# A Mamba layer and its experts on one core: input with channels on rows, the skip term on GpSimd, TensorE busy before its first weights

## The chip, the cores and the metric

The kernel runs on one core of a Trainium2 chip, in one launch and in fp32. The metric is the device time of an execution in microseconds (us), the median over several runs. A profile is of one execution. Engines: PE (TensorE), DVE (VectorE), ACT (ScalarE), POOL (GpSimd) and SP (SyncE, which issues most DMAs). Each works off its own queue of instructions in order, and waits at an instruction until what it needs is there.

## What is computed

Input x is 4 sequences of 1024 tokens with 128 channels. Cut to what matters:

```python
# Mamba: 256 inner channels, 16 states, rank 64, causal convolution over 4 tokens
xr, z = split(x @ W_in.T)                # 256 and 256
xs    = silu(conv(xr, conv_w) + conv_b)
dt_r, b, c = split(xs @ W_x.T)           # 64, 16, 16
dt    = softplus(dt_r @ W_dt.T + b_dt)
for t in range(1024):                    # for each channel and each of 16 states
    h = exp(dt_t * -exp(A_log)) * h + dt_t * xs_t * b_t
    y_t = sum over states (h * c_t) + D * xs_t        # D * xs_t: the skip term
x = layernorm(x + (y * silu(z)) @ W_out.T)
# 8 experts of 128 -> 512 -> 128 with gelu, the best 2 of each token, softmax weights
x = layernorm(x + sum over the 2 experts e of weight_e * expert_e(x))
```

## The kernel before

**Units.** The 4096 tokens are cut into ten units, each a stretch of one sequence: two of 256, then 512s, and at the end 384 and 128 (`UNITS`; units 0 to 9). A unit has its tokens along the free axis and the inner channels on rows, as two halves of 128 (index c). If a unit continues a sequence, the state of the recurrence is carried in a small tile (`goes_on`).

**prepare** of a unit runs during the scans of the unit before. `load_x` (L441) brings x with tokens on rows. `project` (L577) transposes it on PE with the identity into PSUM (`pt_x`, L585), and ACT copies it to `xt` (L603), a tile with 3 extra columns in front for the convolution (the halo: zeros at the start of a sequence, else copied from the unit before by ACT, L595). The convolution is folded into the projection: the four taps times W_in (`taps`, multiplied on DVE, L326) are the weights of four matmuls that accumulate in `pxc` (L613); silu on ACT gives `xs`. `pz` (L638) and its silu `zs` (L649) follow. `select` (L658) makes `px`, `xd`, the transposed b (`bt`), c through DRAM (`cd`), `pd` and the first parts of softplus (`ex`); `softplus` (L732) ends it with a polynomial (`sq` on ACT, `q` four times on DVE), then `dt` and `dtx` = dt * xs on DVE.

**step** (L802), 16 a unit, one for each state: PE spreads b over the rows into PSUM (`u`, L824); a DMA spreads c over the rows of `cc`; ACT makes the decay `a`; DVE multiplies dtx by the spread b (`u`, L861) and runs two scans, one for each half (`h`, L880, two buffers of both halves); POOL multiplies by c (`hc`, L895, three buffers); PE transposes hc and accumulates it over the states into `y` in PSUM (L905, tokens on rows); POOL copies the last state where the sequence goes on (`state`, L920).

**The skip term** (`add_skip`, L926) is ahead of the first state's transposes: PE multiplies xs by a diagonal matrix of D (`skip_sb`, made on DVE at the start, L348), 64 matmuls in all (128 records in fp32), and so starts y's accumulation (L937).

**finish_mixer** (L945) multiplies y by zs (`yg`), projects with W_out (`po`), adds x and normalizes (`stats_m`, `rstd_m`), and makes the routing.

**Experts.** Sparse rounds 0 to 7 take units (0,1), 2, 3, ... 8; the last unit is computed densely, with all experts. `dispatch` (L1113) works out on DVE which slot each token takes, ending with its weights (`twin`, L1241), and POOL scatters the tokens to slots in DRAM with indirect DMAs (`xs_slots`, L1262), eight for a unit of 512. `experts` (L1322) reads slots back four blocks of 128 at a time (`xb`), transposes them (`pt_b`), moves them to `xq`, runs both layers (`ph`, `ht`) with weights that each block's expert selects, and weighs the result (`yb`), which a DMA writes out. In rounds below `LATE` ACT makes `xq` (L1350) and `yb` (L1426), from `LATE` on DVE does (L1359, L1428). `combine` (L1484) gathers on POOL (L1495) and adds; `store` normalizes and writes.

**Order.** A planner (`Plan`, L77) lists all operations with an estimated cost, a wished place and an urgency, and `order` (L147) simulates the engines with these estimates to fix the sequence of each engine's queue; `issue` writes it out as it stands. The constants at the top of the file (`UP`, `GATHER`, `PREP_OF`, `D_OF` and others) are its costs and wishes, so to change them changes the order and nothing else.

**At the start**, x of unit 0 is loaded first, the identity is made on POOL, W_in (256 KB) and the taps are loaded, and PE's first instructions are the transposes of x.

Of the kernel before, what the change touches and what calls it, by code (L numbers as in the profile page):

```python
# [18 lines left out]
RUSH = 100.0  # L19
NEAR, LOTH = 0.1, 1.3  # L20

UP = 0.95
GATHER, SCATTER = 1.85, 1.35
N_B = 2
SCAN_ORDER = 1, 0
B_AT, B_URG = 3.6, 29.9
BESIDE = -6.2
PATIENCE = 0.2
N_RUSH = 0
X_AT, X_STEP, X_URG, C_AT, C_URG, D_AT = 1.9, 2.66, 6.2, 4.0, -1.0, -1.9  # L30
A_AT, A_URG, BC_AT, BC_URG = -0.8, -2.3, 4.2, 15.8
PREP, SEL, SOFT, SSTEP = 25.4, 5.3, -0.1, 2.7
L_URG = -1.0
URG, URG2, URG3, URG4 = 52.0, 191.1, 18.3, 0.8
Z_AT, W2_AT, W1_AT, W1_STEP = 11.2, 0.0, 6.8, 3.5

PREP_OF = (-6.7, -1.0, -10.0, 9.5, 1.2, 0.0, -3.0, 5.6, -5.2, 6.9, -3.9, 3.0)
D_OF = (7.9, -3.5, -6.5, 3.3, 6.5, 4.7, -8.1, 5.3, 4.5, 1.7)
X_OF = (-1.9, -7.6, 2.1, 1.3, 0.5, 0.4, 0.8, -16.1, 6.0, -2.5)
C_OF = (-0.2, 5.0, -3.5, -1.3, 8.3, 3.3, 21.1, -2.6, 2.7, 9.1)  # L40
# [5 lines left out]

DENSE = [(9,)]

LATE = 7
EPS = 1e-5  # L50
TOPK = 2

# [199 lines left out]
def tile_mamba_moe_postln(  # L252
# [18 lines left out]
    out: bass.AP,  # L271
):
    nc = tc.nc
    _, _, DM = x.shape
    KC, DI = conv_w.shape
    NS = a_log.shape[0]
    RK = w_dt_t.shape[0]
# [23 lines left out]
    ps_m = ctx.enter_context(tc.tile_pool(name="ps_m", bufs=5 - N_B, space=bass.MemoryType.PSUM))  # L301


    x_first = io.tile([P, NTC, DM], F32, tag="x", name="x_0", bufs=2)
    nc.sync.dma_start(
        out=x_first[:, : UNITS[0][2] // P, :],
        in_=x[0, : UNITS[0][2], :].rearrange("(c p) d -> p c d", p=P),
    )
    ident = const.tile([P, P], F32, name="ident")
    make_identity(nc, ident)  # L310
    w_in_sb = const.tile([P, 2 * DI], F32, name="w_in_sb")
    nc.sync.dma_start(out=w_in_sb, in_=w_in_t)
# [5 lines left out]
    for j, v in ((1, d_skip), (2, b_dt)):  # L318
# [4 lines left out]
    w_dt_sb = const.tile([RK, DI], F32, name="w_dt_sb")  # L323
    nc.sync.dma_start(out=w_dt_sb, in_=w_dt_t)

    nc.vector.tensor_tensor(  # L326
        taps, taps, w_in_sb[:, :DI].unsqueeze(1).to_broadcast([P, KC, DI]), ALU.mult
    )
# [17 lines left out]
    skip_sb = const.tile([P, NDC, P], F32, name="skip_sb")  # L346
    for c in range(NDC):
        nc.vector.tensor_scalar_mul(skip_sb[:, c, :], ident, vecs[:, 1, c : c + 1])  # L348
    ones = const.tile([P, P], F32, name="ones")
    nc.gpsimd.memset(ones, 1.0)  # L350

# [87 lines left out]
    )  # L439

    def load_x(i, st):  # L441
        b, r = rows(i)
        n = size(i)[1]
        st["x"] = t = sb(io, [P, NTC, DM], "x", 2, f"x_{i}")
        if i == 0:
            t.make = lambda: x_first
            dma(lambda: t(), (), [t], 128)
            return
        dma(
            lambda: nc.sync.dma_start(  # L450
                out=t()[:, :n, :], in_=x[b, r, :].rearrange("(c p) d -> p c d", p=P)
            ),
            (),
            [t],
            256,
        )

    def layernorm(src, part, n, name, *dst):

# [112 lines left out]
    dve(0, lambda: nc.vector.tensor_scalar_mul(nega, nega, -1.0), [decay], [decay])  # L572


    last_xt = {}

    def project(i, st):  # L577
        t_n, n = size(i)
        b, first, _ = UNITS[i]
        src = st["x"]  # L580
        pt = psum(f"pt_x{i}")

        def turn():
            for c in range(n):
                nc.tensor.transpose(pt()[:, c * P : (c + 1) * P], src()[:, c, :], ident)  # L585


        xt = sb(seq, [P, HALO + T], "xt", 3, f"xt_{i}")
        if first == 0:
            dve(0, lambda: nc.vector.memset(xt()[:, :HALO], 0.0), (), [(xt, "halo")], port=False)  # L590
        else:
            prev, end = last_xt[i - 1]
            act(
                0,
                lambda: nc.scalar.copy(xt()[:, :HALO], prev()[:, end : end + HALO]),  # L595
                [(prev, "body")],
                [(xt, "halo")],
            )
        last_xt[i] = xt, t_n
        pe(0.12 * n, turn, [src, (xt, "halo")], [pt])  # L600
        act(
            t_n,
            lambda: nc.scalar.copy(xt()[:, HALO : HALO + t_n], pt()[:, :t_n]),  # L603
            [pt],
            [(xt, "body")],
        )
        xs = sb(seq, [P, NDC, T], "xs", 1, f"xs_{i}")
        for c in range(NDC):
            pp = psum(f"pxc_{i}_{c}")

            def mm(c=c, pp=pp):
                for k in range(KC):
                    nc.tensor.matmul(  # L613
                        pp()[:, :t_n],
                        taps[:, k, c * P : (c + 1) * P],
                        xt()[:, k : k + t_n],
                        start=(k == 0),
                        stop=(k == KC - 1),
                    )

            pe(KC * 1.7e-3 * t_n, mm, [xt], [pp], holds=[xs])

            def fxs(c=c, pp=pp):
                nc.scalar.activation(
                    xs()[:, c, :t_n], pp()[:, :t_n], AF.Silu, bias=vecs[:, 0, c : c + 1]
                )

            act(t_n, fxs, [pp], [(xs, c)], SILU)

        zs = sb(seq, [P, NTC, DI], "zs", 2, f"zs_{i}")  # L630
        for h in range((n + 1) // 2):
# [24 lines left out]
        st["zs"], st["xs"], st["xt"] = zs, xs, xt  # L656

    def select(i, st):  # L658
        t_n, n = size(i)
# [142 lines left out]
    def step(i, st, s):  # L802
# [50 lines left out]
            place=place - A_AT,  # L853
            urgent=A_URG,
        )
        h = sb(scan, [P, NDC, T], "h", 2, f"h_{i}_{s}")

        dve(
            2 * t_n,
# [11 lines left out]
        )  # L871
        hc = sb(scan, [P, NDC, T], "hc", 3, f"hc_{i}_{s}")
        if s == 0:
            add_skip(i, st)
        y = st["y"]
        for c in SCAN_ORDER:

            def run(c=c):
# [15 lines left out]
            def times(c=c):  # L894
# [2 lines left out]
                )  # L897

            plan.add(
                "POOL", 0.05 + 2.33e-3 * t_n, times, [(h, c), cc], [(hc, c)], urgent=30.0, port=True  # L900
            )

            def add(c=c):
                for k in range(n):
                    nc.tensor.matmul(  # L905
                        y()[:, k, c * P : (c + 1) * P],
                        hc()[:, c, k * P : (k + 1) * P],
                        ident,
                        is_transpose=True,
                        start=False,  # L910
                        stop=(s == NS - 1),
                        skip_group_check=True,
                    )

            plan.add("PE", 0.12 * n, add, [(hc, c), y], [y], urgent=30.0)
        if goes_on:
            plan.add(
                "POOL",
                0.15,
                lambda: nc.gpsimd.tensor_copy(carry()[:, s, :], h()[:, :, t_n - 1]),  # L920
                [h],
                [(carry, s)],
                urgent=30.0,
            )


    def add_skip(i, st):
        n = size(i)[1]
        st["y"] = y = plan.buf(
            "y", 1, lambda: ps_y.tile([P, NTC, DI], F32, tag="y", name=f"y_{i}")  # L930
        )
        xs = st["xs"]

        def run():
            for k in range(n):
                for c in range(NDC):
                    nc.tensor.matmul(  # L937
                        y()[:, k, c * P : (c + 1) * P],
                        xs()[:, c, k * P : (k + 1) * P],
                        skip_sb[:, c, :],  # L940
                        start=(k % 2 == 0 and c == 0),
                        stop=False,
                        skip_group_check=True,
                    )

        plan.add("PE", 0.48 * n, run, [xs], [y], urgent=30.0)


    def finish_mixer(i, st, at):
# [534 lines left out]
    def combine(i, st, at):  # L1484
# [184 lines left out]
```

## Time and profile before

| | |
|---|---|
| median of 15 runs | 798.04 us (794.72 to 800.02) |
| profiled execution | 796.63 us, of which its span 794.9 us |
| mean clock granted to PE | 0.914 of full speed |
| instructions of PE, DVE, ACT, POOL | 4594, 1036, 843, 637 |
| bytes moved by DMA | 109.20 MB |

In the profile, L12 is line 12 of the kernel. A group's row gives line, engine, operation, `out<-in` by the program's names, partitions x elements, and xcount; then busy time and mean nanoseconds of one; then the idle time of the engine just before them and what ended most of it (`<-`). In the slices the span is cut into 40 equal parts and each digit is the busy share in tenths. A row of a window has its limits and length, the busy time and count of each engine, the clock granted to PE, the mean share of the 16 DMA engines, and GB/s. A row of the waits has who waited for whom, us in total, times, and the longest. A row of a timeline has start, duration and operation, and in brackets the idle time before it. Matmuls of fp32 appear as two records each, of which some are missing.

### The profile page before, as it was taken

What the parts mean: (1) busy time and instruction counts of PE and PEld (TensorE: products, weight loads), DVE (VectorE), ACT (ScalarE), POOL (GpSimd) and SP (SyncE); (2) the same over time, 40 slices, a digit from 0 to 9 for tenths busy, and PEclk for the clock granted to TensorE, in tenths of its full rate; (3) what the DMA queues carried; (4) which work ended last, traced back from release to release, by engine and by line L of the source; (5) the groups of instructions that cost most, each with busy time, mean ns of one, the idle gap of its engine ahead of it and who ended that gap; (6) DMA issues with size and microseconds to landing.
All of it is one profiled execution on the core that took longest, in us unless ns stands there. A gap on an engine that the chain in (4) does not pass through costs nothing. (4 is left out here: it accounts for less than half of the span.)

```text
span 794.9 us, 14284 instructions
## 1 busy us (share of the span) xinstructions
PE 656.9 (83%) x4594; PEld 561.1 (71%) x4594; DVE 657.3 (83%) x1036; ACT 557.9 (70%) x843; POOL 532.5 (67%) x637
## 2 busy tenths in 40 slices
PE   5557838669997999799987896999789998888785
PEld 4446526449875987598766874988588877777785
DVE  2798999999989998999989989998979997984322
ACT  3853855727867887788777888788867867675553
POOL 4356545576646897579939794769686887975604
PEclk9766958869997999899998998899999999999998
DMA  6962313347515664267524633566355566556652
GB/s 201 225 143 54 107 48 111 94 139 229 136 54 141 181 172 120 69 180 195 127 69 129 193 76 115 160 175 159 80 157 175 141 149 177 144 143 179 147 158 41
DMA packets 106120, 109.20 MB, mean 137 GB/s; under 512 B 9640, under 2 KB 72152, under 8 KB 106048
## 3 DMA queue, kind: packets, MB, share of 16 engines
q1 hardware_dynamic: 94384, 99.44, 44.9%
q0 software_dynamic: 11248, 8.33, 5.9%
q8 instruction: 38, 0.62, 0.3%
q10 hardware_dynamic: 416, 0.53, 0.3%
q14 instruction: 34, 0.28, 0.1%
HBM read 87.96 MB, written 18.27 MB: 134 GB/s over the span
## 5 line engine op out<-in xcount | busy, mean ns | idle before, releaser
L895 POOL TENSOR_TENSOR hc<-h,cc 128x512 f32<-128x512 f32 (+3 forms) x320 | 357.6, 1212 | 157.5 <-PE y L905 38.1
L905 PE MATMUL y<-ident,hc 128*128 128x128 f32 x1024 | 172.9, 293 | 48.3 <-POOL hc L895 45.8
L880 DVE TENSOR_TENSOR_SCAN h<-a,state,u 128x512 f32<-128x512 f32 (+3 forms) x192 | 185.4, 1000 | 20.4 <-POOL hc L895 7.2
L847 ACT ACTIVATE a<-dt,nega 128x1024 f32<-128x1024 f32 (+3 forms) x160 | 152.9, 974 | 65.5 <-DVE h L880 60.0
L861 DVE TENSOR_TENSOR u<-dtx,u 128x1024 f32<-128x1024 f32 (+3 forms) x160 | 162.2, 1014 | 22.1 <-PE u L824 9.6
L905 PEld LDWEIGHTS y<-ident,hc 128*128 128x128 f32 x1024 | 124.8, 150 | 77.2 <-POOL hc L895 70.6
L1314 PE MATMUL ph<-w_sb,ht 128*128 x944 | 131.4, 292 | 24.4 <-ACT ht L1303 24.2
L1314 PEld LDWEIGHTS ph<-w_sb,ht 128*128 128x128 f32 x944 | 121.5, 206 | 29.1 <-ACT ht L1303 28.7
L880 DVE TENSOR_TENSOR_SCAN h<-a,u 128x512 f32<-128x512 f32 (+1 forms) x128 | 132.8, 1074 | 10.0 <-POOL hc L895 3.6
L1290 PE MATMUL ph<-xq,w 128*128 128x128 f32 x944 | 125.9, 284 | 15.2 <-DVE pick L1233 3.1
L243 ACT ACT_TABLE_LOAD x105 | 134.7, 1283 | 3.6 <-PEq L1657 1.8
L1290 PEld LDWEIGHTS ph<-xq,w 128*128 128x128 f32 x944 | 116.3, 198 | 21.2 <-issue 6.3
L1495 POOL DMA_INDIRECT acc<-ys_slots,slot_i x62 | 97.9, 1578 | 41.1 <-DVE acc L1555 24.5
L824 PE MATMUL u<-ident,bt 128*128 128x128 f32 x512 | 89.2, 289 | 10.7 <-DVE h L880 10.7
L1303 ACT ACTIVATE ht<-ph 128x512 f32<-128x512 f32 x118 | 66.2, 597 | 23.7 <-PE ph L1290 23.1
L824 PEld LDWEIGHTS u<-ident,bt 128*128 128x128 f32 x512 | 65.1, 147 | 20.5 <-DVE h L880 13.1
L1426 ACT ACTIVATE yb<-ph,xb 128x128 f32<-128x128 f32 x105 | 37.1, 363 | 47.3 <-PE ph L1314 43.8
L1262 POOL DMA_INDIRECT xs_slots<-acc,slot_i x31 | 33.8, 1089 | 46.9 <-DVE twin L1241 13.2
L613 PE MATMUL pxc<-xt,taps 128*128 128x512 f32 (+3 forms) x160 | 60.0, 523 | 3.4 <-ACT xt L603 2.8
L613 PEld LDWEIGHTS pxc<-xt,taps 128*128 128x128 f32 x160 | 29.3, 199 | 24.6 <-issue 17.7
L745 ACT ACTIVATE sq<-ex,shift 128x1024 f32<-128x1024 f32 (+3 forms) x40 | 38.0, 973 | 7.4 <-DVE q L753 6.9
L1262 POOL DMA_INDIRECT xs_slots<-twin,slot_i x31 | 35.6, 1149 | 6.8 <-issue 5.7
(140 smaller groups left out, 706.9 us busy)
## 6 DMA issues: line engine op xcount, KB each, us to landing
w<-w_dram SPq DMA_DIRECT2D x118, 256.0 KB, 3.4
cc<-cd SPq DMA_DIRECT2D x96, 256.0 KB, 3.5
xb<-xs_slots SPq DMA_DIRECT2D x24, 258.0 KB, 4.3
ys_slots<-yb SPq DMA_DIRECT2D x24, 256.0 KB, 2.9
cc<-cd SPq DMA_DIRECT2D x32, 128.0 KB, 2.9
cc<-cd SPq DMA_DIRECT2D x16, 192.0 KB, 3.1
w_sb<-in_w_dram SPq DMA_DIRECT2D x8, 256.0 KB, 5.4
w_own<-in_w_dram SPq DMA_DIRECT2D x8, 256.0 KB, 6.3
```

Source lines behind the costliest of these rows:

```text
L243: load(table)
L613: nc.tensor.matmul(pp()[:, :t_n], taps[:, k, c * P : (c + 1) * P], xt()[:, k : k + t_n], start=(k == 0), stop=(k == KC - 1),)
L824: nc.tensor.transpose(u_sb[:, bank, k * P : (k + 1) * P], bt()[:, k, s : s + 1].to_broadcast([P, P]), ident,)
L847: lambda: nc.scalar.activation(a()[:, :, :t_n], dt()[:, :, :t_n], AF.Exp, scale=nega[:, s : s + 1]),
L861: nc.vector.tensor_tensor((u_sb[:, 1:3, :t_n] if bank else u_sb[:, 1::-1, :t_n]), dtx()[:, :, :t_n], u_sb[:, bank : bank + 1, :t_n].to_bro ...
L880: nc.vector.tensor_tensor_scan(h()[:, c, :t_n], a()[:, c, :t_n], u_sb[:, (1, bank)[c], :t_n], 0.0 if first == 0 else carry()[:, s, c : c + 1],
L895: nc.gpsimd.tensor_tensor(hc()[:, c, :t_n], h()[:, c, :t_n], cc()[:, :t_n], ALU.mult)
L905: nc.tensor.matmul(y()[:, k, c * P : (c + 1) * P], hc()[:, c, k * P : (k + 1) * P], ident, is_transpose=True, start=False, stop=(s == NS - 1),
L1262: ins = nc.gpsimd.indirect_dma_start(out=rd["xs"]()[:, :], out_offset=bass.IndirectOffsetOnAxis(ap=slot_i()[:, k, st["chunk"] + c : st["ch ...
L1290: nc.tensor.matmul(ph()[:, k * P : (k + 1) * P], w()[:, k * P : (k + 1) * P], xt()[:, width], start=True, stop=True, skip_group_check=True,)
L1314: nc.tensor.matmul(py, ht[:, k, :], w2_sb[:, bass.ds(e, 1), k * DM : (k + 1) * DM].rearrange("p o d -> p (o d)"), start=(k == 0), stop=(k ...
L1495: nc.gpsimd.indirect_dma_start(out=acc()[:, c, :DM], out_offset=None, in_=ys()[:, :], in_offset=bass.IndirectOffsetOnAxis(ap=slot_i()[:, k ...
```

## The change

- x comes with channels on rows (128 x 1024 for each sequence), and a DMA brings a unit's columns straight into `xt`, with the 3 columns before it where the sequence continues. The transposes `pt_x`, ACT's copies and its halo copies go.
- The skip term: POOL multiplies `xs` by D in place (two halves), and adds it to the two halves of the first state's `hc`. PE's diagonal matmuls and `skip_sb` go, and the first state's transposes start y's accumulation.
- `h` has three buffers instead of two.
- `LATE` is 6 instead of 7: round 6's `xq` and `yb` go from ACT to DVE.
- At the start 48 transposes of the identity into a scratch tile stand on PE ahead of its first weights; W_in is loaded in two halves, and the taps are multiplied in two halves.
- A gather reads from the rows of the round's blocks alone.
- The planner's constants and some costs are others, so the order differs on every engine.

```diff
-UP = 0.95
-GATHER, SCATTER = 1.85, 1.35
+UP = 0.97
+SKIP = 1.2e-3
+N_WARM = 48
+GATHER, SCATTER = 1.65, 1.25
...
-PREP_OF = (-6.7, -1.0, -10.0, 9.5, 1.2, 0.0, -3.0, 5.6, -5.2, 6.9, -3.9, 3.0)
+PREP_OF = (-11.6, -6.6, -14.9, 12.2, 0.2, 0.0, -6.2, 4.9, -4.7, 4.1, 7.3, 1.4)
...
-LATE = 7
+LATE = 6
...
-    x_first = io.tile([P, NTC, DM], F32, tag="x", name="x_0", bufs=2)
+    x_first = seq.tile([P, KC - 1 + T], F32, tag="xt", name="xt_0", bufs=3)
     nc.sync.dma_start(
-        out=x_first[:, : UNITS[0][2] // P, :],
-        in_=x[0, : UNITS[0][2], :].rearrange("(c p) d -> p c d", p=P),
+        out=x_first[:, KC - 1 : KC - 1 + UNITS[0][2]], in_=x[0, :, : UNITS[0][2]]
     )
...
-    nc.sync.dma_start(out=w_in_sb, in_=w_in_t)
+    for h in range(2):
+        hs = slice(h * DI, (h + 1) * DI)
+        nc.sync.dma_start(out=w_in_sb[:, hs], in_=w_in_t[:, hs])
+
+    warm = ps_m.tile([P, T], F32, tag="mm", name="warm")
+    for k in range(N_WARM):
+        nc.tensor.transpose(warm[:, k % 4 * P : (k % 4 + 1) * P], ident, ident)
...
+    for c in range(NDC):
+        cs = slice(c * P, (c + 1) * P)
+        nc.vector.tensor_tensor(
+            taps[:, :, cs], taps[:, :, cs],
+            w_in_sb[:, cs].unsqueeze(1).to_broadcast([P, KC, P]), ALU.mult,
+        )
...
+            dma(
+                lambda: nc.sync.dma_start(
+                    out=xt()[:, HALO - back : HALO + t_n], in_=x[b, :, first - back : first + t_n]
+                ),
...
-        h = sb(scan, [P, NDC, T], "h", 2, f"h_{i}_{s}")
+        h = sb(scan, [P, NDC, T], "h", 3, f"h_{i}_{s}")
...
         if s == 0:
-            add_skip(i, st)
+            for c in range(NDC):
+                def scale(c=c):
+                    nc.gpsimd.tensor_scalar_mul(
+                        st["xs"]()[:, c, :t_n], st["xs"]()[:, c, :t_n], vecs[:, 1, c : c + 1]
+                    )
...
+            if s == 0:
+                def skip(c=c):
+                    nc.gpsimd.tensor_tensor(
+                        hc()[:, c, :t_n], hc()[:, c, :t_n], xs()[:, c, :t_n], ALU.add
+                    )
...
-                        start=False,
+                        start=(s == 0 and k % 2 == 0 and c == SCAN_ORDER[0]),
...
-                        in_=ys()[:, :],
+                        in_=ys()[: rd["blocks"] * P, :],
...
-        "x": get("L0_attn_x"),
+        "x": get("L0_attn_x").transpose(0, 2, 1),
```

More of the change, by code (lines that the diff above doesn't have):

```diff
@@ L20 @@
 NEAR, LOTH = 0.1, 1.3
-UP = 0.95
-GATHER, SCATTER = 1.85, 1.35
+UP = 0.97
+SKIP = 1.2e-3
+N_WARM = 48
+GATHER, SCATTER = 1.65, 1.25
 N_B = 2
 SCAN_ORDER = 1, 0
[L26 to L35, printed above, removed]
-PREP_OF = (-6.7, -1.0, -10.0, 9.5, 1.2, 0.0, -3.0, 5.6, -5.2, 6.9, -3.9, 3.0)
-D_OF = (7.9, -3.5, -6.5, 3.3, 6.5, 4.7, -8.1, 5.3, 4.5, 1.7)
-X_OF = (-1.9, -7.6, 2.1, 1.3, 0.5, 0.4, 0.8, -16.1, 6.0, -2.5)
-C_OF = (-0.2, 5.0, -3.5, -1.3, 8.3, 3.3, 21.1, -2.6, 2.7, 9.1)
+B_AT, B_URG = 5.7, 35.9
+BESIDE = -10.2
+PATIENCE = 3.9
+N_RUSH = 2
+X_AT, X_STEP, X_URG, C_AT, C_URG, D_AT = 9.1, 1.65, 12.8, 4.7, 0.8, -3.2
+A_AT, A_URG, BC_AT, BC_URG = 4.3, -0.8, -1.5, 28.5
+PREP, SEL, SOFT, SSTEP = 25.4, 5.6, 0.0, 4.8
+L_URG = -1.7
+URG, URG2, URG3, URG4 = 47.7, 92.4, 22.8, -1.0
+Z_AT, W2_AT, W1_AT, W1_STEP = 11.1, 1.8, 4.7, 5.1
+PREP_OF = (-11.6, -6.6, -14.9, 12.2, 0.2, 0.0, -6.2, 4.9, -4.7, 4.1, 7.3, 1.4)
+D_OF = (20.9, -4.6, -9.5, 10.0, 15.8, -4.4, -4.0, 9.3, -5.6, 4.9)
+X_OF = (-1.7, -8.6, 2.0, 1.0, 0.4, -1.6, 1.0, -16.6, 2.9, -0.4)
+C_OF = (-8.3, -6.8, -2.3, 0.9, 4.3, 3.3, 32.6, -3.4, 7.3, 10.0)
 UNITS = [
@@ L273, in tile_mamba_moe_postln @@
     nc = tc.nc
-    _, _, DM = x.shape
+    _, DM, _ = x.shape
     KC, DI = conv_w.shape
@@ L324, in tile_mamba_moe_postln @@
     nc.sync.dma_start(out=w_dt_sb, in_=w_dt_t)
-    nc.vector.tensor_tensor(
-        taps, taps, w_in_sb[:, :DI].unsqueeze(1).to_broadcast([P, KC, DI]), ALU.mult
-    )
+    for c in range(NDC):
+        cs = slice(c * P, (c + 1) * P)
+        nc.vector.tensor_tensor(
+            taps[:, :, cs],
+            taps[:, :, cs],
+            w_in_sb[:, cs].unsqueeze(1).to_broadcast([P, KC, P]),
+            ALU.mult,
+        )
     w_out_sb = const.tile([P, NDC, DM], F32, name="w_out_sb")
@@ L344, in tile_mamba_moe_postln @@
         nc.gpsimd.memset(shift[:, j : j + 1], b)
-    skip_sb = const.tile([P, NDC, P], F32, name="skip_sb")
-    for c in range(NDC):
-        nc.vector.tensor_scalar_mul(skip_sb[:, c, :], ident, vecs[:, 1, c : c + 1])
     ones = const.tile([P, P], F32, name="ones")
@@ L441, in load_x @@
     def load_x(i, st):
-        b, r = rows(i)
-        n = size(i)[1]
-        st["x"] = t = sb(io, [P, NTC, DM], "x", 2, f"x_{i}")
+        b, first, t_n = UNITS[i]
+        st["xt"] = xt = sb(seq, [P, HALO + T], "xt", 3, f"xt_{i}")
         if i == 0:
[L446 to L456, printed above, removed]
+            xt.make = lambda: x_first
+            dma(lambda: xt(), (), [(xt, "body")], 128)
+        back = HALO if first else 0
+        if not first:
+            dve(0, lambda: nc.vector.memset(xt()[:, :HALO], 0.0), (), [(xt, "halo")], port=False)
+        if i:
+            dma(
+                lambda: nc.sync.dma_start(
+                    out=xt()[:, HALO - back : HALO + t_n], in_=x[b, :, first - back : first + t_n]
+                ),
+                (),
+                [(xt, "body")] + [(xt, "halo")] * (back > 0),
+                256,
+            )
     def layernorm(src, part, n, name, *dst):
@@ L572, in tile_mamba_moe_postln @@
     dve(0, lambda: nc.vector.tensor_scalar_mul(nega, nega, -1.0), [decay], [decay])
-    last_xt = {}
     def project(i, st):
         t_n, n = size(i)
[L579 to L606, printed above, removed]
+        xt = st["xt"]
         xs = sb(seq, [P, NDC, T], "xs", 1, f"xs_{i}")
@@ L655, in project @@
             act(m * DI, fzs, [pp], [(zs, h)], SILU)
-        st["zs"], st["xs"], st["xt"] = zs, xs, xt
+        st["zs"], st["xs"] = zs, xs
     def select(i, st):
@@ L873, in step @@
         if s == 0:
-            add_skip(i, st)
-        y = st["y"]
+            st["y"] = plan.buf(
+                "y", 1, lambda: ps_y.tile([P, NTC, DI], F32, tag="y", name=f"y_{i}")
+            )
[3 more added lines that the diff above has]
+                        st["xs"]()[:, c, :t_n], st["xs"]()[:, c, :t_n], vecs[:, 1, c : c + 1]
+                    )
+                plan.add(
+                    "POOL",
+                    0.05 + SKIP * t_n,
+                    scale,
+                    [(st["xs"], c)],
+                    [(st["xs"], c)],
+                    place=place - 0.5,
+                    urgent=30.0,
+                )
+        y, xs = st["y"], st["xs"]
         for c in SCAN_ORDER:
@@ L899, in step @@
             plan.add(
-                "POOL", 0.05 + 2.33e-3 * t_n, times, [(h, c), cc], [(hc, c)], urgent=30.0, port=True
+                "POOL", 0.08 + 2.4e-3 * t_n, times, [(h, c), cc], [(hc, c)], urgent=30.0, port=True
             )
+            if s == 0:
+                def skip(c=c):
+                    nc.gpsimd.tensor_tensor(
+                        hc()[:, c, :t_n], hc()[:, c, :t_n], xs()[:, c, :t_n], ALU.add
+                    )
+                plan.add(
+                    "POOL",
+                    0.05 + 2.33e-3 * t_n,
+                    skip,
+                    [(hc, c), (xs, c)],
+                    [(hc, c)],
+                    urgent=30.0,
+                    port=True,
+                )
             def add(c=c):
@@ L913, in add @@
                     )
-            plan.add("PE", 0.12 * n, add, [(hc, c), y], [y], urgent=30.0)
+            plan.add("PE", 0.12 * n, add, [(hc, c), y] if s else [(hc, c)], [y], urgent=30.0)
         if goes_on:
@@ L918, in step @@
                 "POOL",
-                0.15,
+                0.32,
                 lambda: nc.gpsimd.tensor_copy(carry()[:, s, :], h()[:, :, t_n - 1]),
@@ L924, in step @@
             )
[L927 to L946, printed above, removed]
     def finish_mixer(i, st, at):
```

## The prediction

> **What bounds the kernel now.** I read the busy table and the slices first, then busy time by window, then the waits of VectorE (DVE) in its long middle, then the groups of instructions that the change touches, and last the timelines of the start and of the last dispatch.
>
> ```profile
> PE 656.9 (83%) x4594; PEld 561.1 (71%) x4594; DVE 657.3 (83%) x1036; ACT 557.9 (70%) x843; POOL 532.5 (67%) x637
> DVE  2798999999989998999989989998979997984322
> POOL 4356545576646897579939794769686887975604
> ```
>
> PE and DVE tie at 83%, but DVE's digits are 9 from the third slice to the last but four, and low only at both ends. The windows (time, PE, PEld, DVE, ACT, POOL busy, clock, DMA) cut the span at the first product `u` and at unit 8's late scans:
>
> ```profile
> 0.00:29.07 29.07, 15.83 (x70) 12.52 (x70) 8.21 (x15) 13.90 (x26) 9.20 (x35) 1.00 0.74 214
> 29.07:240.00 210.93, 160.34 (x917) 123.50 (x918) 192.56 (x282) 132.13 (x185) 121.43 (x163) 0.81 0.43 117
> 240.00:720.00 480.00, 423.20 (x3147) 372.18 (x3145) 435.09 (x668) 376.23 (x565) 369.80 (x405) 0.95 0.54 143
> ```
>
> From 29 to 720 DVE is busy 91% (192.56 of 210.93, 435.09 of 480); most of the rest is gaps of about 0.1 us between its instructions. It is the bound there, and these are its waits proper, from 30 to 720:
>
> ```profile
> DVE u L861 <- PE u L824: 9.3, 8, 3.4
> DVE h L880 <- POOL hc L895: 4.4, 2, 3.6
> DVE h L880 <- POOL state L920: 3.8, 2, 3.3
> DVE stats_m L466 <- PE po L1002: 3.4, 3, 2.0
> ```
>
> So three stages: a prologue of 29.07 us (a chain), 700 us of scans limited by DVE, and a tail of some 61 us (from 734) where round 7 and the dense unit hang on PE and DMA. Work taken off PE, ACT or GpSimd (POOL) is worth only the DVE waits that it ends.
>
> **The skip leaves PE; the first y transposes start the sum.** The groups that go:
>
> ```profile
> L937 PE MATMUL y<-skip_sb,xs 128*128 128x128 f32 x128 | 16.9, 285 | 2.0 <-DVE yg L959 2.0
> L585 PE MATMUL pt_x<-ident,x 128*128 128x128 f32 x32 | 5.5, 286 | 6.0 <-DMA x<-in_x_dram 5.8 <-ACT dt L721 0.2
> L603 ACT COPY xt<-pt_x 128x512 f32<-128x512 f32 (+3 forms) x10 | 4.9, 494 | 1.0 <-PE pt_x L585 1.0
> ```
>
> PE loses 16.9 + 5.5 = 22.4 us. DVE waits for PE 9.3 + 3.4 = 12.7 us in the middle, and one of those waits (1.06 us at 74.8) had a unit's skip products straight in front of `u`. I take a third, −4; from −8 (most go) to +6 (PE's order is new and puts other matmuls in front of `u`; two more waits of the longest, 3.4).
>
> **GpSimd gets it.** 20 scalings of xs by D and 20 additions to the first `hc`. The addition has hc's own shape: 1.25 us at 512, undisturbed. The scaling has no row; below it is the copy of a state (0.34 us), above it the hc product, so 0.6 to 1.25, and I take 1.0 as it has hc's length but one tensor to read. A 512 unit: 2 x 1.25 + 2 x 1.0 = 4.5 us; ten units (3,968 columns against 512 a unit, 7.75 such units) about 35 us, and POOL goes from 67 to 71%. DVE's step is 3.77 us there (u 1.23, two scans 2.33, gaps), POOL's 2.5 (two hc), so POOL makes up 1.27 a step, and the lump is worked off in four steps. DVE does not stop while its h buffers last: with a third h buffer it may run one more step (3.77 us) ahead. 4.5 − 3.77 = 0.7 can be felt where POOL had no slack; +1 in all, from 0 to +16.
>
> The Trainium skill ("SBUF — State Buffer", Who interferes with whom) says that DVE and GpSimd share a port pair held exclusively. The trace agrees as far as its hc products of 512 last 1.43 us in the mean and 1.25 undisturbed; by that difference the 40 new instructions would cost some 0.2 us each, 8 us at most, an estimate that is not in the sum.
>
> **The third h buffer** ends DVE's two long waits for POOL (3.57 at 590.8 `<-POOL hc`, 3.34 at 669 behind a dispatch's scatters): each is shorter than a step of its unit and its overlap (3.77, and 3.09 + 1 in the 384 unit). −6.9, say −7; 0 if the skip's lump takes the room.
>
> **LATE 7 to 6** puts round 6's 15 `yb` and 4 `xq` on DVE. The row of DVE's own `yb` (0.351) and of its `xq` (0.81 at 512):
>
> ```profile
> L1428 DVE TENSOR_SCALAR yb<-ph,xb 128x128 f32<-128x128 f32 x13 | 4.6, 351 | 23.5 <-PE ph L1314 20.5 <-ACT xqd L1110 2.4 <-PE pt_b L1343 0.6
> L1426 ACT ACTIVATE yb<-ph,xb 128x128 f32<-128x128 f32 x105 | 37.1, 363 | 47.3 <-PE ph L1314 43.8 <-DMA ys_slots<-yb 1.5 <-ACT ht L1303 1.1
> ```
>
> In the changed program's order 8 yb and 3 xq come before the weights of dispatch 7: 2.8 + 2.4 + 11 gaps of 0.1 = +6.3 us on the bound. This is the sure loss. They can also wait for PE: ACT's yb waited 14.0 us in 17 instances from 640 to 735 (mean 0.82). Unit 9's scans are queued behind them, but stand between most of them too, and give PE time. +1, from 0 to +12.
>
> **The last dispatch.** From the end of dispatch 7's weights (718.2) the order up to the end is the same. One more step of unit 9 and one more `u` stand before it (1.48 + 0.53 = +2.1), one fewer after it: now scatters to 727.3, then five pairs of hc with 2.1 us of waits to 733.7; then four pairs of 0.85 directly behind the scatters, about 2.7 earlier. Sum −0.6.
>
> **The prologue.** x arrives at 5.78, but w_in at 7.08, the taps product ends 8.31, ACT copies xt from 8.87 (held by nega's load until 8.74) and the halo to 9.4. pxc then runs (timelines of PE and DVE):
>
> ```profile
> 9.27 5.55 PE L613 MATMUL pxc<-xt,taps 128*128 128x256 f32 x16 [2.83 <-ACT xt L603]
> 15.52 1.05 PE L937 MATMUL y<-skip_sb,xs 128*128 128x128 f32 x8
> 28.27 0.69 DVE L780 TENSOR_TENSOR dtx<-dt,xs 128x512 f32<-128x512 f32 x1
> 29.07 0.70 DVE L861 TENSOR_TENSOR u<-dtx,u 128x512 f32<-128x512 f32 x1
> ```
>
> Later at 20.84 the same matmul takes 0.24 a record (6 in 1.46), so 16 would take 3.8: here over half run at half speed, though the clock column has 1.00 (it has no event yet). In the changed kernel the data are there at about 7.2 to 7.7 (half a taps product after half of w_in; no transpose, copy or halo), but 48 transposes stand in front on PE, from about 2.8 when the identity is ready. Four cold ones take 1.06; four warm ones 0.60, of which the last has 0.27 of latency, so they follow each other by 0.11. If they lift the clock after 2.2 to 3.9 us (the span of full PE activity before the rises that I found at 38, 72 and 123 us), 10 to 18 are cold and the rest warm: 48 end at 9.2 to 10.1. pxc then ends about 13.0 to 13.9 instead of 14.82, and without skip products (1.05) px is 2 to 2.9 earlier, with ACT free of 0.35 + 0.19 + 0.60 of copies ahead of `ex`; fold of w_own (0.69) is moved in between the q's and gives 0.8 back. −2; best −3.5.
>
> Do transposes lift the clock? The Trainium skill says no ("TensorE: Matmul & The Clock Gate", Part 4: PE-mode transpose: the full clock "doesn't engage" for them). The trace says yes (timeline of PE: start, duration, line; then two windows, whose clock is the last column but two):
>
> ```profile
> 170.58 1.11 PE L905 MATMUL y<-ident,hc 128*128 128x128 f32 x4 [2.10 <-POOL hc L895]
> 171.49 1.06 PE L824 MATMUL u<-ident,bt 128*128 128x128 f32 x4
> 172.35 1.06 PE L905 MATMUL y<-ident,hc 128*128 128x128 f32 x4
> 173.00:173.50 0.50, 0.41 (x2) 0.00 (x1) 0.50 (x2) 0.00 (x0) 0.34 (x1) 0.56 0.99 377
> 173.50:174.00 0.50, 0.00 (x0) 0.00 (x0) 0.50 (x1) 0.00 (x0) 0.50 (x1) 1.00 0.61 221
> ```
>
> After 2.8 us of nothing but transposes the clock goes from 0.50 to 1.00 at 173.4. If the rule held here, 48 cold ones (0.213 each) would end at 13.05 and pxc stay slow: −2 becomes +1.8.
>
> **Nothing for:** x's DMA in the other layout (same bytes, behind 700 us of scans but for the first); rows of the gather's source; ACT, 70% busy: 11 more table loads in the changed order (11 x 1.283 = +14.1) against 4.9 + 1.1 of copies and 8.4 of yb and xq: even. If ACT were late with `a`, each of seven a buffers would have to drain first. A new order of everything is the wide error: ±3.
>
> **Sum:** −4 +1 −7 +6.3 +1 −0.6 −2 = −5.3. Against the profiled execution (796.63; its span 794.9) 791.3. That execution was 1.41 below the median of the runs, so I forecast 792.7 against 798.04.
>
> **The rivals.**
> 1. *Slower, by GpSimd.* Where the lump of 4.5 us meets gathers (1.58 us each, eight a unit) or scatters, the backlog exceeds the third buffer's 3.77 and the scan waits for `hc`. It decides as soon as the extra buffer is used up at most unit starts: then −7 is not earned and five of nine starts pay 1.5 to 2: sum −5.3 + 7 + 8 = +9.7, 807.7. For: slices of 9 for POOL at 16 and 21. Against: 33% idle.
> 2. *Slower, by the in-order wait.* yb wait for PE the whole 12, and `u` waits as before: −5.3 + 11 + 4 = +9.7, again 807.7; half of it, 802.5. Against: scans between them.
> 3. *The warm-up does nothing, PE's relief neither*: −5.3 + 3.8 + 4 = +2.5, 800.5; with a u wait less, 798: no change.
> 4. *Better:* −8 from PE and −3.5 at the start: 787.
>
> **How the numbers follow.** Forecast and 4 together 0.63; no change 0.09; rivals 1 and 2 with 3's bad end 0.28 (0.13, 0.10, 0.05). A measurement here tells apart about 0.2% (1.6 us), so faster means below 796.4. Own range of the forecast 786 to 796.4; for 8 in 10, which takes in half of rivals 1 and 2, 784 to 804.
>
> **What would show it.** Right: first `u` at about 27; pxc's 16 records in about 3.8 us; no wait `h <- hc` or `h <- state` over 1 us in units 7 and 8; round 6's yb on DVE with short waits. Wrong: `h <- hc` at unit starts, DVE idle `<-PE ph` before unit 9's scans over 5 us, `u <- PE` above 9.3, or a first `u` later than 29.

## The result, and the profile after

The changed kernel takes 810.85 us (median of 9 runs) against 797.55 (median of 46 runs of the kernel before): 1.017 times as long, interval 1.0155 to 1.0186, so 13 us slower where 5 us faster was forecast, and outside the range. The profiled execution has a span of 810.2 us, 15.3 more than before. The experiments ran on four chips on which the kernel before takes 807 to 808; so each is given by its ratio to the kernel before on its own chip, and the changed kernel was timed again beside them (1.0214, 1.0174 to 1.0254).

The page of the changed kernel, its windows, and its DVE waits from 30 to 735 (unit 9 starts later):

```profile
PE 660.8 (82%) x4482; PEld 559.3 (69%) x4482; DVE 664.5 (82%) x1054; ACT 559.2 (69%) x819; POOL 576.8 (71%) x677
DVE  0788888989988999999889999898899988885322
```

```profile
29.00:240.00 211.00, 161.46 (x883) 120.81 (x884) 185.57 (x271) 134.16 (x184) 134.46 (x175) 0.78 0.42 117
240.00:720.00 480.00, 414.27 (x2969) 360.39 (x2968) 436.16 (x640) 369.60 (x541) 394.91 (x427) 0.93 0.52 139
```

```profile
DVE u L843 <- PE u L806: 11.3, 14, 2.1
DVE stats_m L477 <- PE po L998: 6.7, 5, 1.8
DVE over L1170 <- PE cnt L1145: 3.5, 2, 2.6
DVE sc L1053 <- PE pr L1032: 2.8, 4, 1.1
DVE acc L1469 <- PE pb L1457: 2.4, 2, 1.3
DVE h L882 <- POOL state L938: 2.0, 1, 2.0
```

PE lost 22.4 us of work and got 8.1 of warm-up, and is yet busy 3.9 us longer, while its clock in the window to 240 fell from 0.81 to 0.78, in the next from 0.95 to 0.93. DVE's waits for GpSimd (`h <- hc`, `h <- state`) fell from 8.2 to 2.0 us, as forecast. Its waits for PE, counted in these rows, rose from 17.5 (u 9.3, sc 4.8, stats_m 3.4) to 26.7 (the first five). What left one row came back in another.

Followed unit by unit, by the first `u` of each: the first scan starts 1.85 us earlier (27.22 against 29.07), unit 9 starts 8.1 later (698.05 against 689.96), `yg` of unit 9 comes 12.3 later (746.37, 734.11), the end 15.3. So 9.9 us are lost in units 0 to 8, 4.2 in unit 9, 3.0 in the tail. Units 0 and 1 are 2.9 and 3.2 us longer than before, units 2 to 8 between 2.7 shorter and 2.9 longer (unit 2 takes 86.1 in both).

The groups that the change brought to GpSimd, and `yb` on DVE:

```profile
L864 POOL TENSOR_SCALAR xs<-xs,vecs 128x512 f32<-128x512 f32 (+3 forms) x20 | 26.1, 1310 | 22.2 <-DVE dtx L762 20.8
L907 POOL TENSOR_TENSOR hc<-hc,xs 128x512 f32<-128x512 f32 (+3 forms) x20 | 21.1, 1056 | 1.6
L1424 DVE TENSOR_SCALAR yb<-ph,xb 128x128 f32<-128x128 f32 x28 | 9.4, 343 | 29.5 <-PE ph L1310 19.2 <-DMA ys_slots<-yb 3.3 <-ACT xqd L1106 2.4
```

The additions cost what an `hc` costs, as assumed. The scalings take 26.1 us, where 1.0 us at 512 would make 16: at 512 the timeline below has 1.57. Of the 22.2 us that GpSimd stood idle just before them, 17.0 lie ahead of the very first one, in the prologue; so their waiting for `dtx` explains little of what follows.

### The profile page after: what moved, and what is told of

It is laid out like the page before. It is cut to its first block, busy times and chain, and to the rows that moved or that the text cites. A ratio compares the mean times of both kernels' runs of the same rounds, so it can differ in the third digit from the quotient of the medians.

```text
span 810.2 us, 14125 instructions
## 1 busy us (share of the span) xinstructions
PE 660.8 (82%) x4482; PEld 559.3 (69%) x4482; DVE 664.5 (82%) x1054; ACT 559.2 (69%) x819; POOL 576.8 (71%) x677
## 5 line engine op out<-in xcount | busy, mean ns | idle before, releaser
L897 POOL TENSOR_TENSOR hc<-h,cc 128x512 f32<-128x512 f32 (+3 forms) x320 | 351.1, 1196 | 99.3 <-PE y L923 21.0
L923 PE MATMUL y<-ident,hc 128*128 128x128 f32 x1024 | 177.7, 300 | 54.4 <-POOL hc L897 46.4
L923 PEld LDWEIGHTS y<-ident,hc 128*128 128x128 f32 x1024 | 127.3, 153 | 87.2 <-POOL hc L897 76.3
L1310 PE MATMUL ph<-w_sb,ht 128*128 x944 | 136.3, 296 | 27.4 <-ACT ht L1299 27.4
L1310 PEld LDWEIGHTS ph<-w_sb,ht 128*128 128x128 f32 x944 | 124.9, 209 | 34.4 <-ACT ht L1299 32.5
L1286 PEld LDWEIGHTS ph<-xq,w 128*128 128x128 f32 x944 | 117.7, 199 | 20.8 <-ACT xq L1346 8.8
L806 PE MATMUL u<-ident,bt 128*128 128x128 f32 x512 | 91.5, 296 | 16.9 <-DVE h L882 16.9
L806 PEld LDWEIGHTS u<-ident,bt 128*128 128x128 f32 x512 | 67.5, 152 | 26.4 <-DVE h L882 20.0
L1258 POOL DMA_INDIRECT xs_slots<-acc,slot_i x31 | 33.5, 1082 | 44.1 <-DVE rstd_o L491 8.6
L1422 ACT ACTIVATE yb<-ph,xb 128x128 f32<-128x128 f32 x90 | 32.0, 362 | 42.2 <-PE ph L1310 37.8
L864 POOL TENSOR_SCALAR xs<-xs,vecs 128x512 f32<-128x512 f32 (+3 forms) x20 | 26.1, 1310 | 22.2 <-DVE dtx L762 20.8
```

Of the source, the lines that this page charges most:

```text
L806: nc.tensor.transpose(u_sb[:, bank, k * P : (k + 1) * P], bt()[:, k, s : s + 1].to_broadcast([P, P]), ident,)
L897: nc.gpsimd.tensor_tensor(hc()[:, c, :t_n], h()[:, c, :t_n], cc()[:, :t_n], ALU.mult)
L923: nc.tensor.matmul(y()[:, k, c * P : (c + 1) * P], hc()[:, c, k * P : (k + 1) * P], ident, is_transpose=True, start=(s == 0 and k % 2 == 0 ...
L1286: nc.tensor.matmul(ph()[:, k * P : (k + 1) * P], w()[:, k * P : (k + 1) * P], xt()[:, width], start=True, stop=True, skip_group_check=True,)
L1310: nc.tensor.matmul(py, ht[:, k, :], w2_sb[:, bass.ds(e, 1), k * DM : (k + 1) * DM].rearrange("p o d -> p (o d)"), start=(k == 0), stop=(k ...
```

## The experiments

The planner puts every operation anew when one changes. So in most of these kernels it planned as it did, and only what is issued at a place was exchanged: "in its order" means that every engine's queue is the same but for the operations named.

**Undo one part in the new order.** Round 6 back on ACT (`late_on_act`):

```diff
-                lambda: nc.vector.tensor_scalar(
+                lambda: nc.scalar.activation(
+                    xt()[:, : m * P], pt()[:, : m * P], AF.Identity, scale=most, bias=first_only
+                )
+                if r == 6
+                else nc.vector.tensor_scalar(
...
-                if r < LATE:
+                if r < 7:
                     nc.scalar.activation(out, src, AF.Copy, scale=scale)
```

> The changed kernel with every queue in its order, but round 6's 15 yb and 4 xq are issued to ACT where they stood on DVE. Theory LATE (their 6.7 us of DVE work, some 4 us of waits for PE in unit 9, and 3 us in the tail where round 6's gathers come late): 797 to 801. Theories GpSimd, order and clock (the loss sits in units 0 to 8): 807 to 811.

Measured 1.0112 (1.0074 to 1.015). Some 0.6% to 1% comes back of the 1.7% to 2.1%: a part, not the whole.

The skip left out (`no_skip`), and the skip on PE (`skip_on_pe`, the old matmuls in front of the first transposes):

```diff
-                    nc.gpsimd.tensor_scalar_mul(st["xs"]()[:, c, :t_n], ...)
+                    pass
...
-                    nc.gpsimd.tensor_tensor(hc()[:, c, :t_n], hc()[:, c, :t_n], xs()[:, c, :t_n], ALU.add)
+                    pass
```

> The changed kernel with every queue in its order, but the 20 scalings and 20 additions of the skip term on GpSimd are left out (y lacks the skip term). Theory GpSimd (its 47 us hold DVE through hc and PE through y): 800 or less. Theories LATE, order and clock: 809 to 811, the 47 us of GpSimd were under DVE's scans.

Measured 1.0084 (1.0055 to 1.0113): GpSimd's share is 0.9% to 1.3%, 7 to 10 us, and was not under the scans.

> The changed kernel with every queue in its order, but the skip term is again 64 diagonal matmuls on PE, directly in front of the first state's transposes, and not on GpSimd. Theory clock (PE with less to do is granted less clock, so what was taken off PE is given back): no slower than without any skip, 809 to 811, with half-clock time nearer to the 139 us of the kernel before than to the 167 us of the changed one. Theory that PE's load is what DVE waits for: 3 to 8 us above the kernel without a skip.

Measured 1.0164 (1.0131 to 1.0198). On PE, in an order that was not made for it, the skip costs about 6 us more than no skip; GpSimd's 7 to 10 us differ from that by less than the intervals. The theory of the clock had it no slower than without any skip, so that theory falls; nor did PE get more clock (0.887 in the profiled execution, 0.898 without the skip).

**Is it the order?** The constants exchanged, each kernel planned anew (`after_old_order`, `before_new_order`).

> The changed kernel, LATE 6 and all its operations, planned with the old constants and costs. Theory order (the new constants give an order in which PE is late for DVE): 800 to 804. Theory LATE: 808 to 812, the sure work is the same. Both can be blurred by the order that the old constants give to the new operations.

Measured 1.0592 (1.0557 to 1.0628).

> The kernel before, with all of its operations and LATE 7, planned with the new constants and costs. Theory order: 1.01 or above, since the new order is worse by itself. Theory that each set of constants fits its own operations alone: far above, 1.03 to 1.06, as the changed kernel had with the old constants. If the new order costs nothing: 0.995 to 1.003.

Measured 1.0686 (1.0641 to 1.0731). Both are far above: a set of constants fits its own operations only, and neither run says what the new order costs. The next one comes nearer, with the old skip and round 6 in the new order (`new_order_old_ops`):

> The changed kernel with every queue in its new order, but the skip on PE and round 6 on ACT: what differs from the kernel x_direct_h3_warm is then the order of the queues alone. Theory order: 1.007 or more above the kernel before (5 us or more beyond the 1.0015 of x_direct_h3_warm). Theory that LATE and the skip on GpSimd carry all of the loss: 1.000 to 1.004.

Measured 1.0157 (1.0124 to 1.019), as if the order alone carried most of it. But `late_on_act`, with the skip on GpSimd for which this order was made, has 1.0112: parts and order can't be priced apart. What a part costs is what it costs in its queue.

The changed kernel again:

> The changed kernel itself, as the measure for the others on the same chip: 1.015 to 1.019 times the kernel before.

Measured 1.0214 (1.0174 to 1.0254).

**One part alone in the old order.** x straight into xt, with what was transposed and copied left out of its place; with three h buffers, and with the warm-up and the halves (`x_direct_h3_warm`; `x_direct_warm` has two h buffers, `x_direct_h3` has neither the warm-up nor the halves):

```diff
-            for c in range(n):
-                nc.tensor.transpose(pt()[:, c * P : (c + 1) * P], src()[:, c, :], ident)
+            if i > 2:
+                st["fetch"]()          # the DMA of x into xt
...
-        h = sb(scan, [P, NDC, T], "h", 2, f"h_{i}_{s}")
+        h = plan.buf("h", 2, lambda: scan.tile([P, NDC, T], F32, tag="h", name=f"h_{i}_{s}", bufs=3))
```

> The kernel before with every queue in its old order and LATE 7, the skip term on PE, but with x on rows loaded straight into xt (transposes and copies left out of their places), three h buffers, the 48 transposes and the halves of W_in and taps. Theory order (the loss is the new order and round 6 on DVE; these operations are a gain by themselves): 0.987 to 0.993 of the kernel before, 2 us from the start and up to 7 from the third buffer. Theory that some of these operations carry the loss: 1.000 or above.

Measured 1.0015 (0.9996 to 1.0034).

> The same with two h buffers. The difference from the kernel with three is what the third buffer is worth in the old order: 7 us by the prediction (0.009); below 2 us (0.0025) if DVE's waits for GpSimd only move to later waits.

Measured 1.0017 (0.9989 to 1.0044).

> x_direct_h3_warm without the 48 transposes and with W_in and taps in one piece. If the warm-up is worth 2 us to the end: 1.003 to 1.005, with a first u at 28 to 29. If an earlier first u is taken up again by the scans of the first units: 1.001 to 1.002, as with it.

Measured 0.9987 (0.9959 to 1.0016), with a first `u` at 27.63. So in the old order x on rows is worth about nothing at the end, the third buffer 0.0002 where 0.009 was forecast, and the warm-up no gain; all three differences are within the intervals. No run takes the third buffer alone out of the new order. Where the third buffer's gain went is seen in unit 7, where before had a wait of 3.57 for `hc` at 590.80. The kernel with three buffers, DVE and PE:

```profile
591.47 2.33 DVE L895 TENSOR_TENSOR_SCAN h<-a,u 128x512 f32<-128x512 f32 x2
595.67 1.23 DVE L876 TENSOR_TENSOR u<-dtx,u 128x1024 f32<-128x1024 f32 x1 [1.87 <-PE u L839]
593.64 0.66 PE L920 MATMUL y<-ident,hc 128*128 128x128 f32 x4 [0.46 <-POOL hc L910]
595.03 0.60 PE L839 MATMUL u<-ident,bt 128*128 128x128 f32 x4
```

The scan no longer waits for its buffer. But PE takes its queue in order, the transposes of the late `hc` stand in front of the next spread `u`, and DVE waits there. GpSimd's lateness reaches DVE by PE just as well as by the buffers. In all of unit 7, waits for hc went from 3.6 to 0, for u from 1.8 to 3.7, and for pb from 0 to 1.1: 5.4 before, 4.8 after. The same kernel with two buffers (`x_direct_warm`) has the 3.6 and 1.8 of before there. From the first `u` to `yg` of unit 9 its waits for `u` are 20.8 us, with three buffers 29.7, and both take between 717 and 718 us.

Round 6 on DVE (`old_order_late6`), and the skip on GpSimd (`old_order_skip_pool`), each added to `x_direct_h3_warm`:

> x_direct_h3_warm (old order) with round 6's xq and yb issued to DVE where they stood on ACT. Theory LATE (sure work on the bound, and waits for PE that hold unit 9's scans): 1.009 to 1.014 of the kernel before, about 8 us above x_direct_h3_warm. If DVE's waits in unit 9 cover it: 1.001 to 1.004.

Measured 1.0011 (0.9985 to 1.0037): nothing, against 1.0015 without.

> x_direct_h3_warm (old order) with the skip term on GpSimd: two scalings ahead of the first state's hc, an addition behind each half, no matmuls for it on PE. Theory GpSimd (its lump of some 5 us a unit delays hc, then y's transposes on PE, then the spread b that is queued behind them): 1.005 to 1.010. My prediction's price (a gain of 3 us): 0.997 to 0.999.

Measured 1.0369 (1.0337 to 1.0402): 28 us, by far the dearest part. The start of unit 7 in this kernel, GpSimd, PE and DVE:

```profile
557.42 3.70 POOL L919 TENSOR_SCALAR xs<-xs,vecs 128x512 f32<-128x512 f32 x2
573.94 2.33 PE L936 MATMUL y<-ident,hc 128*128 128x128 f32 x8 [2.04 <-POOL hc L922]
576.07 3.48 PE L635 MATMUL pxc<-xt,taps 128*128 128x384 f32 x8
579.82 0.60 PE L846 MATMUL u<-ident,bt 128*128 128x128 f32 x4
580.46 1.23 DVE L883 TENSOR_TENSOR u<-dtx,u 128x1024 f32<-128x1024 f32 x1 [7.45 <-PE u L846]
```

The scalings, the additions and the gathers between them put GpSimd behind; PE stands idle at y for `hc`, its other work (`pxc`) is pushed behind that, and `u` behind both. One such chain costs DVE 7.45 us. From the first `u` to `yg` of unit 9 this kernel takes 30 us longer than `x_direct_h3_warm`; DVE's waits for PE at `u`, `sc` and `stats_m` make 15.5 of them (38.3, 10.1 and 5.4 against 29.7, 5.1 and 3.5). The rest is not traced to one wait.

**Scaling or addition?** The 20 scalings on ACT, at the same places (`old_order_scale_act`, and `after_scale_act` for the changed kernel):

```diff
-                    nc.gpsimd.tensor_scalar_mul(
-                        st["xs"]()[:, c, :t_n], st["xs"]()[:, c, :t_n], vecs[:, 1, c : c + 1]
+                    nc.scalar.activation(
+                        st["xs"]()[:, c, :t_n], st["xs"]()[:, c, :t_n], AF.Copy, scale=vecs[:, 1, c : c + 1]
                     )
```

> old_order_skip_pool with the 20 scalings on ACT instead of GpSimd, the 20 additions stay on GpSimd. It stood at 1.037. Theory that the length of GpSimd's lump decides (3.7 of 6.2 us a unit are scalings): 1.008 to 1.020. Theory that the mere order hc, addition, hc, addition in front of y decides: 1.030 or above.

Measured 1.0204 (1.0176 to 1.0233): of the 28 us 13 go with the scalings. The other 15 stay with the additions on GpSimd or the scalings on ACT, which no run parts in this order.

> The changed kernel with every queue in its order and the 20 scalings on ACT instead of GpSimd. It stood at 1.017 to 1.021, and at 1.008 without any skip. Theory that the lump's length decides: 1.011 to 1.015. If the scalings had been free, done while GpSimd waited for the first h: no change.

Measured 1.0056 (1.0037 to 1.0076). In the new order the scalings are all of GpSimd's price, as far as the intervals tell: without them the kernel is no slower than without any skip (1.0084), and 9 to 13 us faster than the changed one. This is how they act, first in the changed kernel (GpSimd, PE, DVE, and a window with the clock of PE as the last column but two), then with the scalings on ACT:

```profile
169.16 1.57 POOL L864 TENSOR_SCALAR xs<-xs,vecs 128x512 f32<-128x512 f32 x1
171.95 1.55 POOL L864 TENSOR_SCALAR xs<-xs,vecs 128x512 f32<-128x512 f32 x1
173.48 4.94 POOL L897 TENSOR_TENSOR hc<-h,cc 128x512 f32<-128x512 f32 x4
172.01 1.11 PE L923 MATMUL y<-ident,hc 128*128 128x128 f32 x4 [0.80 <-POOL hc L897]
174.78 1.11 PE L923 MATMUL y<-ident,hc 128*128 128x128 f32 x4 [0.81 <-POOL hc L897]
176.55 1.06 PE L806 MATMUL u<-ident,bt 128*128 128x128 f32 x4
177.64 1.23 DVE L843 TENSOR_TENSOR u<-dtx,u 128x1024 f32<-128x1024 f32 x1 [1.81 <-PE u L806]
182.36 1.23 DVE L843 TENSOR_TENSOR u<-dtx,u 128x1024 f32<-128x1024 f32 x1 [0.93 <-PE u L806]
170.00:179.00 9.00, 7.39 (x34) 6.51 (x33) 6.52 (x7) 4.12 (x5) 8.41 (x7) 0.50 0.45 132
```

```profile
163.36 7.59 POOL L900 TENSOR_TENSOR hc<-h,cc 128x512 f32<-128x512 f32 x6
172.70 2.51 POOL L900 TENSOR_TENSOR hc<-h,cc 128x512 f32<-128x512 f32 x2 [1.75 <-PE pt_b L1342]
177.73 1.23 DVE L843 TENSOR_TENSOR u<-dtx,u 128x1024 f32<-128x1024 f32 x1
170.00:179.00 9.00, 8.19 (x74) 8.18 (x75) 8.54 (x7) 6.61 (x9) 5.88 (x5) 1.00 0.56 160
```

These are the scalings of unit 3, yet unit 3 starts at 209.73. They are in GpSimd's queue as soon as `dtx` has read xs, in the middle of unit 2, right behind dispatch 0's scatters, when several `hc` are owed. Without them GpSimd has caught up 7.59 us after the last scatter (170.95) and waits; with them it takes 12.95 (165.47 to 178.42), and DVE loses 2.7 waiting for `u`. PE's clock is also still at half here, where it is full with the scalings on ACT, so that four transposes take 1.11 us and not 0.60; how much of the wait is GpSimd's lateness and how much the slower PE, no run parts. With the scalings on ACT unit 2 takes 82.1 us; in the changed kernel it takes 86.5 in the profile taken beside the experiments and 86.1 in the first. That is some 4 of the 9 to 13 us. Where the others go is not settled: beside the experiments units 5 and 7 are longer too (89.4 and 83.9 against 83.8 and 80.8), but in the first profile (83.9 and 80.2) and in `late_on_act` (85.5 and 80.7), both with the scalings on GpSimd, they lose little or nothing.

**Without the skip, and with half of it on PE** (both from `x_direct_h3`).

> x_direct_h3 (old order, x on rows, three h buffers, no warm-up) with the skip term left out altogether. The difference to x_direct_h3 (0.9987 of the kernel before) is what the skip costs on PE in the order made for it. If PE's 16.9 us were under DVE's scans: 0.997 to 0.999. If they stand in front of the spread b: 0.990 to 0.995, as leaving the skip out of the new order gave 0.013.

Measured 0.9976 (0.9956 to 0.9996): in the order made for it, the skip on PE costs 0.001, about 1 us and less than the intervals tell. There was next to nothing to win by taking it away.

> x_direct_h3 with the skip as a scaling of xs by D on ACT and transposes on PE in place of the diagonal matmuls (one pass instead of two): PE has 8 us less. If PE's share counts: 0.994 to 0.997. If ACT's 20 scalings in front of the decays a hold the first scans of each unit: 1.000 to 1.005. It could beat both kernels.

Measured 1.0017 (1.0002 to 1.0032): no gain. (In some units xs is scaled before others have read it, so part of the recurrence is another one; the instructions are those described.)

**The scalings and round 6 both on ACT**, then without the warm-up too.

> The changed kernel in its order with the 20 scalings on ACT (1.0056 alone) and round 6's xq and yb on ACT too (1.0112 alone, against 1.017 to 1.021 for the changed kernel). If the two prices add: 0.993 to 0.999, it beats both kernels. If the time that the one gives back is taken by the wait behind the other: 1.001 to 1.006.

Measured 1.003 (1.0003 to 1.0057).

> The same without the 48 transposes (W_in and taps stay in halves). If the warm-up is worth 2 us to the end: 0.0025 above the one with it, first u about 2 us later. If, as in the old order, the scans of the first units take it up: within 0.001, or a little below.

Measured 1.0002 (0.9978 to 1.0026). Without the scalings on GpSimd, round 6 on DVE and the warm-up, the rest of the change neither costs nor gains anything that the interval shows. The only version here whose interval lies below the kernel before is the one in the old order that leaves the skip out.

## Why the prediction was wrong

**GpSimd gets it: +1. This is the step that failed, and it had the path wrong.** It let the lump reach DVE through the h buffers alone (4.5 − 3.77 = 0.7), and be worked off in four steps. The runs show another path: late `hc` holds y's transposes on PE, and the spread `u` stands behind them in PE's queue. In the old order the lump stands where I put it, within 4.4 us of its unit's first `u`, and it costs 28 us. In the new order the scalings of units 1 to 8 stand in the unit before, some of them right behind scatters, when GpSimd has no slack to give; there they cost 9 to 13 us, and the additions nothing that shows. 33% idle over the span said nothing on those stretches. The size was off as well: a scaling at 512 takes 1.57 us, not 1.0, so a lump is 5.7 us, not 4.5. (The ten units have 4,096 columns, not 3,968; that sum is not part of the +1.)

Rival 1 had the engine right and put the price at 807.7, but looked for it in waits for `hc`; the rows show it as `u <- PE`. At 0.13 its chance was far too small. Its slices of 9 were misread: they are 15, 19, 20, 22, 24, 28 and 35. The 8 us that the prediction kept aside for DVE and GpSimd in each other's way are not seen: DVE's scans and `u` last 1.001 and 1.014 us in the mean (1.000 and 1.014 before), `hc` 1.196 (1.212 before).

**The third h buffer: −7.** The waits for GpSimd went as said (8.2 to 2.0 us), and the time did not: in the old order, where it was tried alone, the buffer gained nothing, as it was not the only link from GpSimd to DVE. Nowhere in this step did the prediction ask what is late next. The answer was on the page of before: PE's `y` waits for `hc` 45.8 us in all, and `u` is in the same queue.

**PE relieved: −4.** Taken from a third of DVE's waits for PE, of which the prediction's list left out one (`sc` for `pr`, 4.8 us). Without any skip the old order gains 0.001. So PE's 16.9 us lay where DVE hardly waited for them, and in the rows above the waits for PE came from what PE itself waits for.

**LATE: +6.3 and +1.** Between nothing (old order) and 0.6% to 1% (new order, alone), 0.3% with the scalings gone and with intervals that overlap. The 6.7 us of work are there (4.4 yb, 2.3 xq in unit 9, against busy time), but of unit 9's 44.1 us before the change DVE had been busy for 30.1 only and idle for 14.0 (DVE is the third of the engines in the row):

```profile
689.96:734.11 44.15, 38.15 (x297) 33.44 (x297) 30.11 (x98) 30.11 (x61) 30.96 (x53) 1.00 0.62 161
```

"On the bound" was true from 29 to 720 as a mean, not there. Rival 2 is not seen: in unit 9 of the changed kernel `yb` waits 4.0 us in all, none of it for `ph`. Why the tail is 3.0 us longer is not settled: round 6's gathers start late there, after a wait of 9.80 us for round 6's last `yb`, but with round 6 on ACT the tail was no shorter (65.0 us from `yg` of unit 9 to the end, against 63.8).

**The last dispatch: −0.6.** The order came as said: four pairs of `hc` directly behind the scatters, and `yg` 5.6 us after the last scatter instead of 6.8. That is 1.3 us earlier, where about 2.7 was said; the tail behind `yg` is 3.0 us longer for all that.

**The prologue: −2.** Right at its place: first `u` 1.85 us earlier. It did not last, and one of its parts delays it. With and without the 48 transposes, in the last two kernels:

```profile
2.81 7.17 PE L319 MATMUL warm<-ident 128*128 128x128 f32 x48 [2.81 <-POOL ident masks.py:199]
9.82 3.62 PE L595 MATMUL pxc<-xt,taps 128*128 128x256 f32 x16
```

```profile
6.83 5.65 PE L595 MATMUL pxc<-xt,taps 128*128 128x256 f32 x16 [6.83 <-DVE taps L335]
```

The transposes make pxc 2.03 us shorter and start it 2.99 later: its end moves from 12.48 to 13.44, the first `u` from 25.30 to 26.26. (To the end of the kernel the two differ by 0.003, and their intervals overlap.) I had both numbers (data ready at 7.2 to 7.7, the transposes' end at 9.2 to 10.1), and compared with the old start at 9.27 instead of the new one. What the start gained, unit 0 gave back: it takes 42.6 us instead of 39.7. The new order has pxc of unit 1 not at 20.8 but in the scans, on a PE that had stood idle for 10 us:

```profile
32.67 3.36 PE L595 MATMUL pxc<-xt,taps 128*128 128x256 f32 x8
36.29 0.70 DVE L843 TENSOR_TENSOR u<-dtx,u 128x512 f32<-128x512 f32 x1 [2.09 <-PE u L806]
```

**Order as ±3.** Far too small: the constants alone, with the same operations, moved the kernel before by 6.9% (1.0686) and the changed one by about 4% (1.0592 against 1.017 to 1.0214).

## What to carry to other kernels

An engine with a third of its time idle can still hold the bound: look at the queue where the new work will stand, not at the share, and count whom the in-order queues behind it serve. A buffer that ends a wait may gain nothing while a second path (here `hc` to `y` to `u` on PE) carries the same lateness. And an order fitted to one set of operations prices every change against it: compare parts with the queues held fixed, and do not expect a moved operation to cost its duration: 26 us of scalings cost 9 to 13 here, 6.7 us of round 6 between nothing and 8.

## What the runs showed of the hardware

GpSimd's scaling of one fp32 tensor by a value per row took 1.57 us at 128x512, longer than its product of two tensors (1.25 to 1.27); ACT's took 0.63 in the mean over all shapes (`after_scale_act`), against 1.31 on GpSimd (the changed kernel).

Transposes lift the clock of PE here: 48 of them took 7.17 us, where 48 at the slow 0.213 would take 10.2, and after them pxc's 16 records took 3.62 us, without them 5.65. The Trainium skill ("TensorE: Matmul & The Clock Gate", Part 4: PE-mode transpose) says the opposite, that the full clock doesn't engage in that mode; the runs decide. In both these kernels the clock column has 1.00 in the first 20 us, so in that stretch the speed is read from the durations, not from the column.

In the changed kernel the clock fell soon after PE went idle: PE's last prologue work ends at 18.95, and the clock of the stretch from 20 to 25 is 0.70, which is full speed up to 22, about 3 us of idling.
